# Two score buffers instead of one, and token-sum blocks of x read earlier, in a masked self-attention kernel

## The chip, the cores and the metric

The kernel runs on one core of a Trainium2 chip. A core has five engines that run their own instruction streams and wait for each other by semaphores: PE (matrix products, results only into PSUM), DVE (vector work), ACT (elementwise functions, here above all the exponentials), POOL (here it issues the row gathers and scatters) and SP (here it issues the other transfers). PSUM has eight banks; one bank holds 512 float32 values per partition. Times are device microseconds of one execution; the time of a kernel is the median of its runs.

## The reference

```python
xt = jnp.transpose(x, (0, 2, 1))                    # x: (16, 512, 1024), float32
q = xt @ Wq.T                                       # 512 x 512
qh = q.reshape(B, T, 8, 64).transpose(0, 2, 1, 3)   # 8 heads of 64
scores = scale * jnp.einsum('bhqd,bhkd->bhqk', qh, qh)
logits = (scores * cmask + (1.0 - cmask) * NEG) * rmask
attn = jax.nn.softmax(logits, axis=-1)
ctx = jnp.einsum('bhqk,bhkd->bhqd', attn, qh)
out = ctx.transpose(0, 2, 1, 3).reshape(B, T, D) @ Wo.T
return x + jnp.transpose(out, (0, 2, 1))
```

Queries, keys and values are the same projection. The mask has about half of the 1024 tokens of a batch on. A token that is on attends only to the tokens that are on. A token that is off has logits of zero everywhere, so its row is the plain mean over all tokens of the batch: this is why the kernel needs sums of x over all tokens.

## The kernel before, in words

The kernel sorts the tokens of each batch into slots: the tokens that are on come first, and 512 to 544 slots ("A") are computed. The four blocks of 128 slots are gathered as rows of x (`gather`, an indirect transfer on POOL, tile `xa`), the few slots beyond 512 are the "tail" (tile `xt`). Float32 products are made from float16 halves: each operand is split into a high and a low part, and three products are added.

The 16 batches are worked in a software pipeline, in the loop `for b in range(B + 1)` of `run`. While batch b has its scores and products made, batch b + 1 has its queries made and batch b + 2 is gathered, scaled, split and transposed. Each turn of the loop has eight stages, `st` 0 to 7. A stage is: `scores` of the head pair st // 2 and the half st % 2; then what is listed in `side[st]`; then what is listed in `fill[st]`. PE's order is that of the text, since each product is chained behind the one before (`then`). The other engines' orders come from the framework's scheduler: it goes by the order of the text, but an instruction that is ready while its engine is free can go ahead of earlier ones that aren't. Some work is put into queues with a cost and a due time (`drip`: lines T, D, A, X) and leaves them as the text advances.

`scores` (from L852) makes 12 matmuls for two blocks of 128 keys (k = 0, 1) and two heads (h = 0, 1), three products for each, the six of block 0 first. Each block and head has a PSUM bank of its own, 128 keys x 512 queries. Four exponentials on ACT (L870) follow in the order of the blocks; they write the tiles `p`. All four banks belong to one PSUM tile, `S` (profile name `pss`); the other four banks are the rotating tiles `pm`. The same banks are used by `tail_scores` (the scores of the tail, exponentials on L940), by one transpose in `xt` for the first batch, and by two of the four output products in `last`:

```python
self.S = self.ps_s.tile([P, 4 * 512], F32, tag="s", name="pss")
bank = lambda k, h: self.S[:, (2 * h + k) * 512:(2 * h + k + 1) * 512]
```

`attend(b, p)` multiplies the exponentials of a head pair by the values (tiles `v`); it comes two stages after the pair's first scores. Its last products use `pt` (and `pu` for the wider batches), the tail's exponentials, which go through DRAM (`td`) and come back by SP transfers (L972, L973). The reciprocals of the softmax sums are transposed on PE, copied (`rr`, L1042), written to DRAM (`rd`, L1044) and read back spread over partitions (`rb`, L1053 and L1057); DVE multiplies the result by them in `norm_scale` (L1086).

The values `v` of batch b + 1 come from the query halves `hl` by transposing transfers on SP (L707), two for each head pair; DVE adds the two parts (L719), ACT squares them (L735). The gathered rows are scaled and split into tiles `xs` (two buffers; ACT L626, DVE L627) and transposed by SP into `X` (L628). DVE's `range_now` (L566) reads `X` whole.

The token sums: for batch a = b + 2, x itself lies in DRAM as 512 features x 1024 tokens. `load_all(a, c)` reads the block of 128 features c (512 KB, SP, L541) into a tile `xm`, which has two buffers; `sum_half(a, c)` queues an ACT instruction (L529) that sums each row into a column of `ms2`. When all four are there, `mean_x` (L647, L552, L553) writes the means as one more column of `X`. In batch b the four reads stand in `fill[0]` to `fill[3]` and the four sums in `side[2]` to `side[5]`:

```python
for c in range(DC):
    fill[2 * c // 2].append(L(self.load_all, a, c, None if b else first_top))
    side[c + 2 if b else (2, 2, 3, 4)[c]].append(L(self.sum_half, a, c))
```

Of the kernel before, what the change touches and what calls it, by code (L numbers as in the profile page):

```python
# [10 lines left out]
F32 = mybir.dt.float32  # L11
# [3 lines left out]
AF = mybir.ActivationFunctionType  # L15
# [4 lines left out]
P = 128  # L20
D = 512
T = 1024
H = 8
DK = 64
NP = H // 2
DC = D // P
TB = T // P
SCALE = 0.125
# [23 lines left out]
class Fast:  # L52
# [12 lines left out]
    def __init__(self, ctx, tc, x, x_nat, mask_t, wq_t, wo_t, out):  # L65
        self.tc, self.nc = tc, tc.nc
        self.x, self.x_nat, self.out = x, x_nat, out
        self.B = B = x.shape[0] // T
        self.wide = [512 if b in (0, B - 2, B - 1) else C if b < 5 else 528 for b in range(B)]
        pool = lambda name, bufs, **k: ctx.enter_context(tc.tile_pool(name=name, bufs=bufs, **k))  # L70
        self.const = pool("const", 1)
        self.one = pool("one", 1)
        self.dram = pool("dram", 8, space=bass.MemoryType.DRAM)
        self.ps_s = pool("ps_s", 1, space=PS)
        self.ps_m = pool("ps_m", 4, space=PS)
        self.S = self.ps_s.tile([P, 4 * 512], F32, tag="s", name="pss")
        self.st = {}
        self.last_pe = None
        self.scatters = []
        self.exp, self.pool = [], []  # L80

        self.paced, self.beat = False, None
        self.urgent, self.spare = [], []

        self.lines, self.credit, self.rates = {k: [] for k in RATES}, {k: 0.0 for k in RATES}, dict(RATES)
        self.idle, self.now, self.many, self.pair = 0.0, 0.0, 9, 1
        self.w, self.raw = {}, {}
        self.src = {"q": wq_t, "o": wo_t}
        self.setup(mask_t)
# [503 lines left out]
    def xt(self, b, k):  # L593

        nc, s = self.nc, self.st[b]
        A = s["A"]
        n = P if k < 4 else A - 512
        if k == 0:
            self.need(("r", b - 2))
        if k == 3 and b > 1:  # L600
            self.drip(("x", b), 0.1, lambda: self.mean_x(b), "X", 5.0)
        if n:
            x = s["xa"][k] if k < 4 else s["xt"]
            if b == 0:
                if k == 3:
                    s["cut"] = {}
                    for i, (y, r) in {3: (x, P)}.items():
                        z = s["cut"][i] = self.sb([P, D], F32, "tmp", 2)
                        with self.behind(self.last_xa):
                            nc.scalar.activation(z[:r], y[:r], AF.Copy, scale=self.hit[:r, b, i:i + 1])  # L610
                if k > 2:
                    x = s["cut"][k]
                pt = (self.S[:, :DC * n] if k == 3 else self.pm([P, DC * n])).rearrange("p (c n) -> p c n", c=DC)
                for c in range(DC):
                    self.tr(pt[:, c, :], x[:n, c * P:(c + 1) * P], self.ident[:n, :n])
                self.last_xt = self.pe
                self.xsplit(b, (slice(None), slice(None), slice(k * P, k * P + n)), pt)
            else:
                self.drip(("x", b), 0.9, lambda: self.turn_x(b, k, n, x), "X")
# [232 lines left out]
    def scores(self, b, p, half, between=None):  # L852

        nc, s = self.nc, self.st[b]
        self.sums(b)
        hl = s["hl"][p]
        bank = lambda k, h: self.S[:, (2 * h + k) * 512:(2 * h + k + 1) * 512]
        for k in range(2):
            if between and k:
                between()  # L860
            block = slice((2 * half + k) * P, (2 * half + k + 1) * P)
            for m, (t, u) in enumerate(((0, 0), (0, 1), (1, 0))):
                for h, rows in enumerate((slice(0, DK), slice(DK, P))):
                    self.beat = self.mm(bank(k, h), lhsT=hl[rows, t, block], rhs=hl[rows, u, :512], start=(m == 0), stop=(m == 2)).ins
        self.exp = []
        for k in range(2):
            i = 2 * half + k
            x = self.sb([P, 2, C], F32, "p", PB)
            for h in range(2):
                self.exp = [nc.scalar.activation(x[:, h, :512], bank(k, h), AF.Exp, bias=s["nm"][:, 2 * p + h:2 * p + h + 1], scale=SCALE,  # L870
                                                 accum_out=s["z"][:, 2 * p + h, i:i + 1]).ins]
                s["ps"][p, i, h] = x[:, h]
            if s["nt"]:
                s["blocks"].append((p, i, x))
        self.tail_columns(b)
        self.after(1.7 if b else 4.0)
# [42 lines left out]
    def tail_scores(self, b):  # L919

        nc, s = self.nc, self.st[b]
        A, n = s["A"], s["nt"]
        if not n:
            return
        self.sums(b)
        w = 2 * n
        per = P // w
        for j in range(NP // per):
            o = 1024 * j + 512 - A // 2
            for x, y in self.pieces(o, A):  # L930
                for m, (t, u) in enumerate(((0, 0), (0, 1), (1, 0))):
                    for r in range(per):
                        e = j * per + r
                        self.beat = self.mm(self.S[r * w:(r + 1) * w, o + x:o + y], lhsT=s["tk"][:, e, t, :], rhs=s["hl"][e][:, u, x:y],
                                            start=(m == 0), stop=(m == 2)).ins
        s["tp"] = self.sb([P, 2, C], F32, "p", PB)
        for j in range(NP // per):
            o = 1024 * j + 512 - A // 2
            t = s["tp"][:, j, :A]
            nc.scalar.activation(t, self.S[:, o:o + A], AF.Exp, bias=s["nm"][:, H + j:H + j + 1], scale=SCALE,  # L940
                                 accum_out=s["zt"][:, j:j + 1])
            self.drip(("th", b), 1.0, lambda j=j, t=t: self.tail_halves(b, j, t), "T", 1.0 + 0.9 * j)

# [256 lines left out]
    def last(self, b):  # L1200

        s = self.st[b]
        self.paced = False
        self.attend(b, 3)
        pos = [self.S[:, i * 512:(i + 1) * 512] for i in range(2)] + [self.pm([P, 512]) for _ in range(2)]
        part = lambda i, es: self.product(s["ch"], s["cl"], slice(i * P, (i + 1) * P), pos[i], es)
        part(0, range(3))
        self.recip_last(b, 3)
        part(2, range(3))
        part(1, range(3))  # L1210
        while self.urgent or self.spare:
            self.issue()
        for i in (0, 2, 1):
            self.project(b, i, pos[i], range(3, DC))
        part(3, range(3))
        self.project(b, 3, pos[3], range(3, DC))

    def run(self, flag):
        B = self.B
# [79 lines left out]
        first_top = self.st[0]["top"]  # L1299
# [5 lines left out]
        L = lambda f, *a: lambda: f(*a)  # L1305
        Q = lambda n, e, g: L(self.query, n, e, g)
        for b in range(B + 1):
            o, n, a = b - 1, b + 1, b + 2
# [8 lines left out]
            fill = [[] for _ in range(8)]  # L1317
            side = [[] for _ in range(8)]
# [28 lines left out]
            if n < B:  # L1347
# [40 lines left out]
                if b:  # L1388
                    fill[7] += [L(self.top, n, ALL), L(self.bottom, n, ALL)]
                else:  # L1390
                    fill[7] += [L(self.warm, 40), L(self.top, n, ALL)]
            if a < B:
                self.start(a)
                for c in range(DC):
                    fill[2 * c // 2].append(L(self.load_all, a, c, None if b else first_top))
                    side[c + 2 if b else (2, 2, 3, 4)[c]].append(L(self.sum_half, a, c))
                if not b or any(b == g[0] - 2 for g in groups):
                    fill[0 if b else 1] += [L(self.hot, a)]
                else:
                    side[0] += [L(self.hot, a)]  # L1400
                fill[1 if b else 3] += [L(self.index, a)] + [L(self.gather, a, j) for j in range(5 if self.wide[a] > 512 else 4)]
                for k, st in enumerate((4, 5, 6, 6, 7) if b else (4, 4, 5, 6, 6)):
                    side[st].append(L(self.xt, a, k))
# [43 lines left out]
def general_batch(tc, pools, consts, b, x, mask, out):  # L1447
# [5 lines left out]

    xt = big.tile([P, TB, D], F32, name="g_xt")
    nc.sync.dma_start(out=xt, in_=x[bs].rearrange("o (j p) d -> p (o j) d", p=P))
    cm = big.tile([P, T], F32, name="g_cm")
    nc.scalar.dma_start(out=cm, in_=mask[bs].broadcast_to([P, T]))
# [131 lines left out]
```

## Time and profile before

| | before |
|---|---|
| median of 3 runs | 907.66 us (907.16 to 910.43) |
| profiled execution | 904.99 us |
| its span, first to last instruction | 903.3 us |
| mean granted PE clock | 0.991 |
| PE busy | 867.2 us (96%) |
| DVE busy | 646.9 us (72%) |
| ACT busy | 630.5 us (70%) |
| POOL busy | 295.7 us (33%) |

A row of the wait table reads: engine, tile and line that waited, what ended the wait, total us, times, longest. A row of a window reads: stretch, its length, busy us and number of instructions of PE, PEld (weight loads), DVE, ACT and POOL, granted PE clock, share of the DMA engines, GB/s. A busy PE is one with a matmul in flight; matmuls overlap, so the sum of their durations is more than their busy time. SP has no work of its own: its rows are transfers at the time when they are issued, not when they land.

### The profile page before, as it was taken

To read this page: it belongs to the slowest core of one execution; us is meant where nothing else is said; L and a number is where in the kernel's file an instruction comes from. 1 tells how busy PE (TensorE), PEld (TensorE's weight loads), DVE (VectorE), ACT (ScalarE), POOL (GpSimd) and SP (SyncE) were. 2 spreads that over 40 slices of the span, in tenths; PEclk is the share of its full clock that TensorE was granted. 3 is DMA by queue.
4 is the path that set the end of the run, shared out by engine and by line. 5 is a ranking of instruction groups with operands and counts; after the bars stand their busy time and mean duration, and the time that the engine had idled before them with its cause. 6 is when DMAs were issued, how large, how long until landed. Compare 5 with 4: busy or idle time off the path is not lost.

```text
span 903.3 us, 20115 instructions
## 1 busy us (share of the span) xinstructions
PE 867.2 (96%) x7149; PEld 500.1 (55%) x7149; DVE 646.9 (72%) x2027; ACT 630.5 (70%) x1667; POOL 295.7 (33%) x309
## 2 busy tenths in 40 slices
PE   6788999999999999999999999899999999999896
PEld 5565655556565465655555565464655556464443
DVE  7656877867758677787856888586777877655662
ACT  5868786777767768686866868577676867766640
POOL 3201111222122322243443334242432433345673
PEclk9899999999999999999999999999999999999999
DMA  6957766769769888987979988698996979686652
GB/s 189 251 107 169 160 164 162 167 136 209 178 146 191 196 183 215 201 209 192 228 199 219 198 206 215 152 216 202 200 220 156 220 202 222 166 175 161 204 197 110
DMA packets 193129, 169.24 MB, mean 187 GB/s; under 512 B 145135, under 2 KB 155629, under 8 KB 193021
## 3 DMA queue, kind: packets, MB, share of 16 engines
q1 hardware_dynamic: 171836, 100.20, 52.2%
q0 software_dynamic: 21184, 67.68, 24.8%
q8 instruction: 58, 0.95, 0.5%
q14 instruction: 51, 0.41, 0.2%
HBM read 97.30 MB, written 38.51 MB: 150 GB/s over the span
## 4 chain that ended last, share of the span: by engine, by line
PE 83%; DMA 8%; ACT 4%; DVE 3%; issue 1%; POOL 0%; SPq 0%; POOLq 0%; DVEq 0%; ACTq 0%
PE pm L107 61%; PE pss L107 20%; DMA X<-xs 3%; ACT p L870 2%; PE pm L110 1%; DMA pu<-td 1%; DMA xa<-x_in,idx 1%; DMA pt<-td 1%; DMA rb<-rd 1%; DMA v<-hl 1%; ACT xs L626 0%; POOL xa L492 0%; DVE xa L1178 0%; DVE xs L627 0%; DVE xa L1114 0%
## 5 line engine op out<-in xcount | busy, mean ns | idle before, releaser
L870 ACT ACTIVATE p<-pss,nm 128x512 f32<-128x512 f32 x512 | 346.3, 686 | 149.0 <-PE pss L107 133.5
L107 PE MATMUL pm<-p,v 128*64 128x264 f32 (+2 forms) x2048 | 243.6, 391 | 0.5 <-DVE hl L672 0.4
L107 PE MATMUL pss<-hl 64*128 64x512 f16 x1536 | 193.3, 383 | 10.9 <-ACT p L870 8.4
L107 PEld LDWEIGHTS pm<-p,v 128*64 128x64 f32 x2048 | 141.7, 137 | 95.2 <-issue 16.0
L107 PE MATMUL pm<-X,wqh 128*128 128x264 f16 (+5 forms) x1024 | 177.5, 277 | 2.4 <-DMA X<-xs 2.1
L107 PE MATMUL pm<-X,wql 128*128 128x264 f16 (+5 forms) x512 | 141.6, 276 | 0.0
L492 POOL DMA_INDIRECT xa<-x_in,idx x68 | 71.8, 1055 | 204.0 <-DVE idx L393 70.2
L107 PEld LDWEIGHTS <-hl 64*128 64x128 f16 (+1 forms) x1568 | 69.9, 95 | 100.2 <-issue 36.9
L1191 POOL DMA_INDIRECT y_out<-xa,idx x68 | 70.3, 1034 | 132.6 <-DVE xa L1114 28.3
L107 PEld LDWEIGHTS <-wqh 128*128 128x128 f16 x1024 | 96.7, 98 | 29.8 <-issue 14.9
L870 ACT ACTIVATION_READ_ACCUMULATOR p<-pss,nm 128x1 f32 x512 | 103.9, 203 | 0.0
L1191 POOL DMA_INDIRECT y_out<-xi,idx x56 | 65.4, 1168 | 109.8 <-PE pss L107 30.0
L492 POOL DMA_INDIRECT xi<-x_in,idx x56 | 56.5, 1010 | 114.3 <-PE pss L107 55.4
L107 PE MATMUL pm<-woh,ch 128*128 128x512 f16 x240 | 91.4, 381 | 0.0
L107 PE MATMUL pm<-woh,cl 128*128 128x512 f16 x240 | 91.0, 379 | 0.1
L107 PE MATMUL pm<-wol,ch 128*128 128x512 f16 x240 | 91.0, 379 | 0.0
L672 DVE SCALAR_TENSOR_TENSOR hl<-pm,hl 128x264 f16<-128x264 f32 (+5 forms) x128 | 54.8, 428 | 31.2 <-ACT hl L671 30.8
L107 PEld LDWEIGHTS <-ch 128*128 128x128 f16 x480 | 43.4, 98 | 59.4 <-issue 15.6
L671 ACT ACTIVATE hl<-pm 128x264 f16<-128x264 f32 (+5 forms) x128 | 51.0, 398 | 29.7 <-PE pm L107 29.5
L529 ACT ACTIVATE xm<-xm 128x1024 f32<-128x1024 f32 (+1 forms) x60 | 62.4, 1041 | 2.7 <-DMA xm<-x_nat_in 2.7
L1086 DVE TENSOR_TENSOR c<-c,rb 128x528 f32<-128x528 f32 (+2 forms) x60 | 42.0, 703 | 26.1 <-DMA rb<-rd 24.7
L566 DVE TENSOR_REDUCE top<-X 128x1 f32<-128x529 f16 (+4 forms) x64 | 44.1, 695 | 20.7 <-DMA X<-xs 15.8
(237 smaller groups left out, 1158.6 us busy)
## 6 DMA issues: line engine op xcount, KB each, us to landing
xm<-x_nat_in SPq DMA_DIRECT2D x56, 512.0 KB
rb<-rd SPq DMA_DIRECT2D x28, 512.0 KB
ub<-ud SPq DMA_DIRECT2D x16, 256.0 KB
pt<-td SPq DMA_DIRECT2D x27, 132.0 KB
td<-th SPq DMA_DIRECT2D x9, 264.0 KB
td<-th SPq DMA_DIRECT2D x8, 272.0 KB
pt<-td SPq DMA_DIRECT2D x8, 272.0 KB
xi<-x_nat_in SPq DMA_DIRECT2D x8, 256.0 KB
```

Source lines behind the costliest of these rows:

```text
L107: return self.then(self.nc.tensor.matmul(out, lhsT=lhsT, rhs=rhs, start=start, stop=stop))
L110: return self.then(self.nc.tensor.transpose(out, x, ident))
L492: dma = self.nc.gpsimd.indirect_dma_start(out=tile[:n], out_offset=None, in_=self.x, in_offset=bass.IndirectOffsetOnAxis(ap=idx, axis=0))
L529: self.nc.scalar.activation(s["xm"][k], s["xm"][k], AF.Copy, accum_out=s["ms2"][:, k:k + 1])
L566: self.once(nc.vector.tensor_reduce(s["top4"][:, c:c + 1], self.X[b % 2][:, c, :s["A"] + min(b, 2) % 2 + min(b, 1)], AX.X, ALU.max, apply_ ...
L671: self.last_hl = nc.scalar.activation(hl[:, 0, cols], pq, AF.Copy, scale=1.0 / (SX * SW)).ins
L672: nc.vector.scalar_tensor_tensor(hl[:, 1, cols], pq, 1.0 / (SX * SW), hl[:, 0, cols], ALU.mult, ALU.subtract)
L870: self.exp = [nc.scalar.activation(x[:, h, :512], bank(k, h), AF.Exp, bias=s["nm"][:, 2 * p + h:2 * p + h + 1], scale=SCALE, accum_out=s[" ...
L1086: self.once(nc.vector.tensor_tensor(c[:, :A], c[:, :A], s["rp"][p] if "rp" in s else s["rb"][:, p, :A], ALU.mult), self.beat)
L1191: dma = self.nc.gpsimd.indirect_dma_start(out=self.out, out_offset=bass.IndirectOffsetOnAxis(ap=idx, axis=0), in_=x, in_offset=None)
```

## The change

The one PSUM tile of four banks becomes two tiles of two banks, `S[0]` and `S[1]`, one for each block of 128 keys; within a tile, the bank is that of the head. `tail_scores` uses one of them for each of its runs, and `xt` and `last` use `S[0]`. The number of banks is the same.

For batches from the third on, the reads c = 0 and 1 of batch b + 3 are listed in `fill[6]` and `fill[7]` of turn b, where they stood in `fill[0]` and `fill[1]` of turn b + 1. The reads c = 2 and 3 go from `fill[2]` and `fill[3]` to `fill[1]` and `fill[2]`. The sums go from `side[2]` to `side[5]` to `side[0]`, `side[1]`, `side[3]` and `side[4]`. The first turn keeps its places for batch 2.

```diff
-        self.S = self.ps_s.tile([P, 4 * 512], F32, tag="s", name="pss")
+        self.S = [self.ps_s.tile([P, 2 * 512], F32, tag="s%d" % k, name="pss") for k in range(2)]
...
-                pt = (self.S[:, :DC * n] if k == 3 else self.pm([P, DC * n])).rearrange("p (c n) -> p c n", c=DC)
+                pt = (self.S[0][:, :DC * n] if k == 3 else self.pm([P, DC * n])).rearrange("p (c n) -> p c n", c=DC)
...
-        bank = lambda k, h: self.S[:, (2 * h + k) * 512:(2 * h + k + 1) * 512]
+        bank = lambda k, h: self.S[k][:, h * 512:(h + 1) * 512]
...
-            o = 1024 * j + 512 - A // 2
+            o = 512 - A // 2
...
-                        self.beat = self.mm(self.S[r * w:(r + 1) * w, o + x:o + y], lhsT=s["tk"][:, e, t, :], rhs=s["hl"][e][:, u, x:y],
+                        self.beat = self.mm(self.S[j][r * w:(r + 1) * w, o + x:o + y], lhsT=s["tk"][:, e, t, :], rhs=s["hl"][e][:, u, x:y],
...
-            nc.scalar.activation(t, self.S[:, o:o + A], AF.Exp, bias=s["nm"][:, H + j:H + j + 1], scale=SCALE,
+            nc.scalar.activation(t, self.S[j][:, o:o + A], AF.Exp, bias=s["nm"][:, H + j:H + j + 1], scale=SCALE,
...
-        pos = [self.S[:, i * 512:(i + 1) * 512] for i in range(2)] + [self.pm([P, 512]) for _ in range(2)]
+        pos = [self.S[0][:, i * 512:(i + 1) * 512] for i in range(2)] + [self.pm([P, 512]) for _ in range(2)]
...
+            if a + 1 < B:
+                self.start(a + 1)
+                for c in range(2):
+                    fill[6 + c].append(L(self.load_all, a + 1, c))
             if a < B:
-                self.start(a)
+                if not b:
+                    self.start(a)
                 for c in range(DC):
-                    fill[2 * c // 2].append(L(self.load_all, a, c, None if b else first_top))
-                    side[c + 2 if b else (2, 2, 3, 4)[c]].append(L(self.sum_half, a, c))
+                    if not b or c > 1:
+                        fill[c if not b else c - 1].append(L(self.load_all, a, c, None if b else first_top))
+                    side[(0, 1, 3, 4)[c] if b else (2, 2, 3, 4)[c]].append(L(self.sum_half, a, c))
```

More of the change, by code (lines that the diff above doesn't have):

```diff
@@ L937, in tail_scores @@
         for j in range(NP // per):
-            o = 1024 * j + 512 - A // 2
+            o = 512 - A // 2
             t = s["tp"][:, j, :A]
-            nc.scalar.activation(t, self.S[:, o:o + A], AF.Exp, bias=s["nm"][:, H + j:H + j + 1], scale=SCALE,
+            nc.scalar.activation(t, self.S[j][:, o:o + A], AF.Exp, bias=s["nm"][:, H + j:H + j + 1], scale=SCALE,
                                  accum_out=s["zt"][:, j:j + 1])
```

## The prediction

> **What bounds the kernel.** I read the page's busy line first, then the waits of the matrix engine (PE), then single stretches of the timeline. The timeline's columns are start, duration, engine, line, operation, tiles, form, count, and in brackets the idle time before it with what ended it.
>
> ```profile
> PE 867.2 (96%) x7149; PEld 500.1 (55%) x7149; DVE 646.9 (72%) x2027; ACT 630.5 (70%) x1667; POOL 295.7 (33%) x309
> PE pss L107 <- ACT p L870: 8.4, 5, 3.1
> 33.50:89.00 55.50, 44.84 (x397) 28.10 (x397) 34.75 (x114) 44.00 (x115) 4.65 (x5) 0.91 0.73 159
> 260.00:580.00 320.00, 313.55 (x2588) 178.02 (x2586) 238.28 (x761) 232.29 (x610) 108.58 (x107) 1.00 0.86 202
> 580.00:835.80 255.80, 255.80 (x2062) 145.41 (x2058) 182.54 (x558) 182.82 (x490) 97.34 (x92) 0.99 0.80 192
> ```
>
> PE is busy 867.2 of 903.3 us and its matmuls stay as they are, so nearly all that can be won are its 36.1 us of idle time. The three windows show where that lies: 10.7 us in the first batch, 6.5 us between 260 and 580, nothing from there to 835.8; the rest is the start before the first scores and the last batch with the end. PE's waits for the exponentials (8.4 us in five) are the largest entry; the single waits follow.
>
> **Part 1, the two score buffers.** First what one tile of four banks does now, in the last batch:
>
> ```profile
> 850.78 1.47 PE L107 MATMUL pss<-hl 64*128 64x512 f16 x12
> 852.17 1.09 PE L107 MATMUL pm<-ident,rcol 128*64 128x128 f32 x16
> 855.18 1.47 PE L107 MATMUL pss<-hl 64*128 64x512 f16 x12 [1.92 <-ACT p L870]
> 845.77 1.47 PE L107 MATMUL pss<-hl 64*128 64x512 f16 x12 [0.24 <-ACT p L870]
> 850.89 0.37 ACT L988 COPY c<-pm 128x256 f32<-128x256 f32 x1 [0.50 <-PE pm L107]
> 852.35 0.69 ACT L870 ACTIVATE p<-pss,nm 128x512 f32<-128x512 f32 x1 [1.09 <-PE pss L107]
> 853.03 0.68 ACT L870 ACTIVATE p<-pss,nm 128x512 f32<-128x512 f32 x1
> 854.35 0.69 ACT L870 ACTIVATE p<-pss,nm 128x512 f32<-128x512 f32 x1
> 89.03 0.82 PE L107 MATMUL pss<-hl 64*128 64x512 f16 x6 [0.42 <-ACT p L870]
> ```
>
> The exponentials begin at 852.35, after all twelve matmuls (850.78 + 1.47 = 852.25), and the next scores begin 0.14 us after the fourth exponential (854.35 + 0.69 = 855.04). So the whole tile is handed over at once, both ways. With a tile for each block, the first pair of exponentials waits for six matmuls (0.82 us with the drain, so 0.65 us sooner), and the first six matmuls of the next stage wait for two exponentials. Here: ACT is free at 851.26, so the exponentials start 0.65 sooner; the second ends at 853.06, the fourth at 854.39. PE is free at 853.26, starts there, does six, waits from 853.91 to 854.39 + 0.14 = 854.53, and ends at 855.35 where it now ends at 856.65: 1.30 us won. The 0.24 before 845.77 goes as well. Together 1.5 us.
>
> In the first batch the same happens:
>
> ```profile
> 42.14 2.75 PE L107 MATMUL pss<-hl 64*128 64x512 f16 x12 [3.08 <-ACT p L870]
> 51.20 0.39 PE L107 MATMUL pm<-X,wqh 128*128 128x274 f16 x2 [2.10 <-DMA X<-xs]
> 75.29 0.67 ACT L870 ACTIVATE p<-pss,nm 128x512 f32<-128x512 f32 x1
> 76.89 0.70 ACT L870 ACTIVATE p<-pss,nm 128x512 f32<-128x512 f32 x1
> 77.73 2.75 PE L107 MATMUL pss<-hl 64*128 64x512 f16 x12 [2.73 <-ACT p L870]
> 79.55 0.72 ACT L626 ACTIVATE xs<-xa,hs 128x512 f16<-128x512 f32 x1 [1.07 <-DMA X<-xs]
> ```
>
> The 3.08 before 42.14 brings nothing: whatever PE wins there it loses at 51.20, where it waits for a transfer that does not depend on these scores. The 2.73 before 77.73 splits. Six matmuls can follow the second exponential (75.29 + 0.67 = 75.96, plus 0.14), the other six still start at 77.73; the end comes at 78.55 and not at 80.48. These twelve took 2.75 us where the others take 1.47, at half rate, and two short stalls with work between may leave the rate whole. But the next exponentials stand behind the split of x at 79.55, which waits for a transfer, so of the 1.9 us some 1.5 remain when the first batch ends. Bounds: 0, if that transfer sets everything, and 4.8 (2.73 + 0.42 + 1.28 + the slow start behind it). I take 1.5, nearest to the worked rows. Part 1 is 3.0 us.
>
> The Trainium skill, page "TensorE: Matmul & The Clock Gate", section "What's actually happening", says that the half rate comes after about one idle window of 3.4 us. The trace differs: half rate after 3.08 and 2.73 us, none after 2.10. By the page's figure the 1.28 us at 77.73 would have another cause and could stay.
>
> The price of part 1 is a wait in the middle of each stage's scores, on ACT. Two starts of six take 2 x 0.82 against 1.47, so 0.17 x 128 = 22 us is the upper end, if the pipeline drains at each; the lower end is 0, if a wait that is already met costs nothing. I take 0, since in most stages the old exponentials are over long before. Behind that wait stands all of PE's queue. On ACT, the first exponentials move forward by 0.65 us in all 128 stages; between 260 and 835 that is cover without value, as PE is full.
>
> **Part 2, the reads of x.** Two of four 512 KB reads per batch move from stages 0 and 1 to stages 6 and 7 of the batch before in the text, the other two one stage forward; the sums move with them. What the SP queue does today is not the text's order:
>
> ```profile
> 524.50 0.39 PE L107 MATMUL pss<-hl 64*128 64x512 f16 x2
> 530.07 1.26 SPq L1053 DMA_DIRECT2D rb<-rd  x2
> 532.75 1.01 SPq L972 DMA_DIRECT2D pt<-td  x2
> 559.84 0.36 SPq L541 DMA_DIRECT2D xm<-x_nat_in  x1
> 560.30 1.23 SPq L707 DMA_TRANSPOSE v<-hl  x1
> 570.93 9.26 SPq L628 DMA_TRANSPOSE X<-xs  x3
> 567.27 0.69 DVE L719 TENSOR_TENSOR v<-v 128x512 f32<-128x512 f16 x1 [3.44 <-DMA v<-hl]
> 577.54 0.72 ACT L626 ACTIVATE xs<-xt,hs 16x512 f16<-16x512 f32 x1 [4.01 <-DMA X<-xs]
> 578.16 0.68 ACT L940 ACTIVATE p<-pss,nm 128x528 f32<-128x528 f32 x1
> 578.98 2.29 PE L107 MATMUL pss<-hl 64*128 64x512 f16 x12 [2.43 <-ACT p L940]
> 581.61 4.40 PE L107 MATMUL pm<-p,v 128*64 128x264 f32 x32
> 498.79 3.78 PE L107 MATMUL pm<-p,v 128*64 128x264 f32 x32
> DVE v L719 <- DMA v<-hl: 21.0, 10, 3.5
> ```
>
> The read of the next batch already goes out at 559.84, five stages early, as soon as a buffer is free: just ahead of the last transpose of v (560.30). DVE then stands 3.44 us for that v, the split of x behind it is late, so is the transpose at 570.93, ACT stands 4.01 us for it, and PE 2.43 us. The restart costs 2.29 - 1.47 = 0.82 in the scores and 4.40 - 3.78 = 0.62 in the products behind: 3.9 us in all. DVE waits like this in ten batches (21.0 us), and one batch earlier the late transpose came out another way:
>
> ```profile
> 476.23 0.70 DVE L566 TENSOR_REDUCE top<-X 128x1 f32<-128x529 f16 x1 [3.75 <-DMA X<-xs]
> 470.68 0.39 PE L107 MATMUL pss<-hl 64*128 64x512 f16 x2
> 481.45 1.13 SPq L972 DMA_DIRECT2D pt<-td  x2
> 477.18 0.39 PE L107 MATMUL pm<-X,wqh 128*128 128x264 f16 x2 [0.29 <-DVE rr L1042]
> 491.50 0.39 PE L107 MATMUL pm<-pt,vt 96*128 96x264 f16 x2 [1.94 <-DMA pt<-td]
> ```
>
> There DVE waited for X, the row of reciprocals and pt went out late, and PE lost 0.29 + 1.94 = 2.2 us. With the sums in stages 0, 1, 3 and 4, the buffers come free one to two stages sooner, the two early reads go out before the last v, and both stalls go: 3.9 + 2.2 = 6.1 us. Bounds: 0 if a read still stands before v, 6.1 if none does; I take the upper end, as DVE's 3.44 us is about one 512 KB read (2.6 us at the 202 GB/s of the window). What is late next at 578.98 is not seen up to 835.
>
> What it costs: the other two reads now come in stages 1 and 2, where the reciprocals (rb), pt and the first v transposes run. On SP they may pass those transposes, whose sums on DVE come some stages later; POOL's queue is not passed, but its gathers share the DMA engines, and those are at 0.86 of their time in the window 260 to 580 above:
>
> ```profile
> 278.59 0.27 PE L107 MATMUL pm<-pu,vt 64*128 64x272 f16 x1 [1.19 <-DMA pu<-td]
> L529 ACT ACTIVATE xm<-xm 128x1024 f32<-128x1024 f32 x56 | 59.9, 1070 | 0.6 <-DMA xm<-x_nat_in 0.6
> ```
>
> If the read goes ahead of pt, PE waits. From 470.68 to pt's issue at 481.45 are 10.8 us, and PE waited 1.94; from 524.50 to 532.75 are 8.3, and it did not. So 2.5 us later costs up to 1.9, and the upper end is 12 batches x 2.0 = 24 us; the lower is 0, if pt goes first, as it does in the text. I take 2.6 us, one read's time, once, in the batch that has no slack (278.59, where PE already waits 1.19). The sums add 2 x 1.07 us to ACT in stages 0 and 1, with its 70% no bound there.
>
> **Sum.** The profiled execution took 904.99 us (span 903.3). 904.99 - 3.0 - 6.1 + 2.6 = 898.5. The median before, 907.66, is 2.67 above that execution, so I predict 901.2.
>
> **Rivals.**
> - Only part 1 shows. The reads go out when buffers are free and not where the text has them, so one may still stand ahead of the last v: 907.66 - 3.0 = 904.7, within 0.5%. For it: the read at 559.84, five stages ahead of its text. Against: the sums, which free the buffers, do move.
> - Slower: the read of stage 1 goes out ahead of rb and pt. SP stands idle before rb at 530.07, which invites it. Then 12 x 2.0 replaces the 2.6: 922.6; in half of the batches it gives 910.6. It decides from 0.8 us a batch on (9.1 / 12). Against: the sum that frees the buffer comes after the exponentials of stage 0, at about the time of rb. The Trainium skill, page "DMA: Bandwidth & Descriptors", section "Queues, rings and completion order", says that each DMA engine takes a ring's descriptors in order; this rival is that rule at work, and 560.30 behind 559.84 agrees with it.
> - The wait inside the scores drains PE: +22 us, 923. Against: only that the old exponentials are mostly over by then; no row shows a met wait inside a run of scores.
>
> **How the numbers follow.** The forecast, both parts at work, has 0.50, with a range of its own of 897 to 903. Only part 1: 0.25. The reads ahead of pt: 0.20, of which 0.13 in so many batches that it is slower by over 0.5%. The drained scores: 0.05. The low end is all gains at their bounds, 907.66 - 4.8 - 1.5 - 6.1, about 895; the high end, 911, takes in pt late in half of the batches. A change under 0.5%, or 4.5 us, is about what can't be told from none. Faster: 0.50; within: 0.25 + 0.07 = 0.32; slower: 0.13 + 0.05 = 0.18.
>
> **What the new profile would show.** Part 1: exponentials starting 0.65 us before the twelve matmuls end, no wait near 855 over 0.7 us. Part 2: DVE's total wait for v well under 21.0, no wait of PE for L940. Wrong: more waits of PE for pt or pu, longer waits of DVE for rb, or pairs of six matmuls taking 1.64.

## The result and the profile after

The changed kernel takes 917.77 us (median; 910.6 to 926.14) against 906.35 us for the kernel before on the same chip: 1.0115 times the time, with a 95% interval of 1.008 to 1.015. The forecast was 901.2 us and faster; it is slower by some 10 us (0.0115 of 906.35), beyond the upper end of the range, 911. The kernel was run again with the experiments: 916.2 against 903.66 us, 1.0127 (1.0092 to 1.0162). One of the first six executions, the profiled one of 926.14 us, was disturbed, so the ratio leaves it out and the rows of the changed kernel below are those of the second run, whose span is 915.3 us against 903.3 before.

The busy line of the page, and the largest waits of PE:

```profile
PE 873.8 (95%) x7149; PEld 498.4 (54%) x7149; DVE 645.5 (71%) x2027; ACT 628.8 (69%) x1667; POOL 305.5 (33%) x309
```

```profile
PE pm L107 <- DMA pt<-td: 5.0, 3, 2.5
PE pss L107 <- ACT p L870: 4.2, 5, 1.8
PE pm L110 <- DVE smcol L793: 4.0, 1, 4.0
...
PE pm L110 <- DVE p L890: 2.8, 3, 1.6
```

PE's wait for the exponentials went from 8.4 to 4.2 us, as part 1 said. New are a wait of 4.0 us for `smcol` (the largest of a head's sums of squares) and waits for `p` at L890; `pt` went from 1.9 to 5.0 us. PE is also 6.6 us longer busy (873.8 against 867.2) with the same 7149 matmuls. Windows by stretch of work, the kernel before first, show where the time went; the borders are the starts of batches 0, 1, 2, 8, 10 and 15:

```profile
33.50:89.00 55.50, 44.84 (x397) 28.10 (x397) 34.75 (x114) 44.00 (x115) 4.65 (x5) 0.91 0.73 159
89.00:144.50 55.50, 55.47 (x455) 32.42 (x454) 43.72 (x128) 43.59 (x113) 8.40 (x8) 1.00 0.65 151
144.50:470.70 326.20, 324.30 (x2635) 183.84 (x2636) 243.51 (x776) 236.79 (x621) 93.30 (x92) 1.00 0.81 189
470.70:579.00 108.30, 103.63 (x867) 59.03 (x867) 80.82 (x263) 77.55 (x204) 38.88 (x38) 1.00 0.90 205
579.00:835.80 256.80, 256.80 (x2068) 145.92 (x2067) 183.54 (x562) 182.82 (x490) 97.34 (x92) 0.99 0.80 192
835.80:903.30 67.50, 58.16 (x431) 29.16 (x430) 36.12 (x89) 25.81 (x75) 40.28 (x37) 0.98 0.52 170
```

```profile
33.60:89.10 55.50, 43.45 (x399) 26.93 (x400) 34.75 (x113) 43.50 (x114) 6.16 (x5) 0.96 0.70 159
89.10:151.90 62.80, 60.29 (x458) 33.76 (x459) 43.83 (x129) 44.28 (x115) 8.08 (x8) 0.92 0.61 138
151.90:478.00 326.10, 325.10 (x2633) 183.10 (x2632) 245.00 (x776) 235.91 (x621) 97.80 (x92) 1.00 0.82 188
478.00:589.10 111.10, 105.91 (x867) 59.37 (x868) 80.63 (x265) 77.40 (x204) 39.32 (x37) 0.98 0.88 200
589.10:848.80 259.70, 256.60 (x2069) 144.66 (x2068) 181.86 (x561) 182.09 (x490) 98.67 (x93) 1.00 0.82 190
848.80:915.30 66.50, 58.33 (x431) 28.73 (x431) 35.19 (x87) 25.66 (x75) 42.52 (x37) 0.97 0.52 173
```

Batch 1 is 7.3 us longer, the two batches where the forecast saw gains 2.8 longer instead of shorter, the full stretch 2.9 longer; the last batch is 1.0 shorter. Batch 1 is the plainest case. The matmuls around its start, and two windows behind it:

```profile
74.48 0.82 PE L107 MATMUL pss<-hl 64*128 64x512 f16 x6 [1.23 <-ACT p L870]
75.81 0.82 PE L107 MATMUL pss<-hl 64*128 64x512 f16 x6 [0.51 <-ACT p L870]
...
88.68 0.45 PE L110 MATMUL pm<-ident,smcol 128*128 128x128 f32 x1 [4.00 <-DVE smcol L793]
```

```profile
88.70:92.70 4.00, 3.88 (x16) 1.34 (x16) 2.09 (x13) 1.85 (x5) 0.00 (x0) 0.50 0.02 4
92.70:96.70 4.00, 4.00 (x25) 2.34 (x27) 2.67 (x5) 3.14 (x11) 0.00 (x0) 0.66 0.11 26
```

Where 2.73 us stood before the scores at 77.73, there are now 1.23 and 0.51, and the scores run at full rate (0.82 us for six). But the gain does not reach the next batch: PE comes sooner to a product for which DVE is not ready, stands 4.00 us in one piece (still inside the first batch's window, whose length stays 55.5 us), and then has a clock of 0.50 for 4 us and of 0.66 for 4 more, which is worth 4.0 x 0.50 + 4.0 x 0.34 = 3.4 us in batch 1. The Trainium skill, page "TensorE: Matmul & The Clock Gate", section "What's actually happening", says half rate after an idle window of about 3.4 us; this wait agrees with it, shorter ones shown below do not.

The rest of batch 1's 7.3 us is a second stall, for the tail's exponentials:

```profile
114.74 0.41 PE L107 MATMUL pm<-pt,vt 128*128 128x272 f16 x2 [2.04 <-DMA pt<-td]
...
115.72 2.57 PE L107 MATMUL pss<-hl 64*128 64x512 f16 x11
```

```profile
113.00:121.00 8.00, 5.92 (x37) 3.32 (x38) 3.64 (x12) 4.37 (x12) 2.05 (x2) 0.79 1.06 148
```

PE waits 2.04 us for `pt` and 0.34 for `pu`, and the clock of 0.79 takes another 8.0 x 0.21 = 1.7 us: 3.4 + 2.4 + 1.7 = 7.5, about what the window shows.

The last batch did what was forecast: its wait of 1.92 us is 0.51.

```profile
866.96 0.82 PE L107 MATMUL pss<-hl 64*128 64x512 f16 x6 [0.51 <-ACT p L870]
```

On DVE two waits have grown, before and after:

```profile
DVE rcol L1021 <- ACT p L870: 13.7, 14, 1.0
DVE sd L738 <- ACT tmp L735: 11.3, 12, 3.6
```

```profile
DVE rcol L1021 <- ACT p L870: 43.3, 17, 4.8
DVE sd L738 <- ACT tmp L735: 33.6, 31, 2.7
```

`rcol` at L1021 is the first step of the softmax sums and needs the last exponential of a batch; `sd` at L738 is the sum of ACT's squares over a head's 64 values (the expectations below call it a maximum). DVE waits 30 and 22 us longer at these two. At `rcol` most of that is an old wait in a new place: DVE's wait at the maximum `m` (L802) for PE falls from 22.4 to 0.9 us, since DVE now stands at the sums first. Nothing in the text of the change concerns these instructions. The order in which DVE's instructions stand has changed: with the two buffers alone, 365 of 2027 instructions of DVE, 74 of 1065 of ACT and 18 of 455 of SP have to be moved to get from one order to the other (the fewest that do it).

### The profile page after: what moved, and what is told of

It reads as the page before. It is cut to its first block, busy times and chain, and to the rows that moved or that the text cites. A ratio compares the mean times of both kernels' runs of the same rounds, so it can differ in the third digit from the quotient of the medians.

```text
span 924.4 us, 20160 instructions
## 1 busy us (share of the span) xinstructions
PE 877.8 (95%) x7149; PEld 501.0 (54%) x7149; DVE 646.3 (70%) x2027; ACT 628.5 (68%) x1667; POOL 301.9 (33%) x309
## 4 chain that ended last, share of the span: by engine, by line
PE 67%; DMA 13%; DVE 8%; ACT 6%; issue 3%; POOL 1%; SPq 1%; POOLq 0%; DVEq 0%; ACTq 0%
PE pm L107 50%; PE pss L107 16%; ACT p L870 3%; DMA X<-xs 3%; DMA rb<-rd 3%; DMA v<-hl 3%; PE pm L110 1%; DMA xa<-x_in,idx 1%; DMA pt<-td 1%; ACT xm L529 1%; ACT xs L626 1%; DMA pu<-td 1%; DVE xs L627 1%; DVE v L719 1%; DVE top L566 1%
## 5 line engine op out<-in xcount | busy, mean ns | idle before, releaser
L870 ACT ACTIVATE p<-pss,nm 128x512 f32<-128x512 f32 x512 | 344.8, 687 | 83.3 <-PE pss L107 54.1
L107 PE MATMUL pm<-p,v 128*64 128x264 f32 (+2 forms) x2048 | 247.8, 396 | 3.6 <-DVE hl L672 3.6
L492 POOL DMA_INDIRECT xa<-x_in,idx x68 | 77.1, 1134 | 210.7 <-DVE idx L393 66.7
L870 ACT ACTIVATION_READ_ACCUMULATOR p<-pss,nm 128x1 f32 x512 | 105.0, 205 | 0.0
L1191 POOL DMA_INDIRECT y_out<-xi,idx x56 | 61.5, 1099 | 121.5 <-PE pm L107 49.9
L492 POOL DMA_INDIRECT xi<-x_in,idx x56 | 60.9, 1088 | 107.6 <-PE pss L107 47.0
L988 ACT COPY c<-pm 128x264 f32<-128x264 f32 (+2 forms) x128 | 43.2, 383 | 54.2 <-PE pm L107 54.0
L738 DVE TENSOR_REDUCE sd<-tmp 128x8 f32<-128x512 f32 x64 | 43.7, 683 | 32.6 <-ACT tmp L735 32.1
L671 ACT ACTIVATE hl<-pm 128x264 f16<-128x264 f32 (+5 forms) x128 | 47.4, 396 | 28.1 <-PE pm L107 28.0
```

Of the source, the lines that this page charges most:

```text
L107: return self.then(self.nc.tensor.matmul(out, lhsT=lhsT, rhs=rhs, start=start, stop=stop))
L492: dma = self.nc.gpsimd.indirect_dma_start(out=tile[:n], out_offset=None, in_=self.x, in_offset=bass.IndirectOffsetOnAxis(ap=idx, axis=0))
L671: self.last_hl = nc.scalar.activation(hl[:, 0, cols], pq, AF.Copy, scale=1.0 / (SX * SW)).ins
L738: nc.vector.tensor_reduce(s["sd"][:, e, :], sq.rearrange("p (k d) -> p k d", d=DK), AX.X, ALU.add)
L988: nc.scalar.copy(c[:, g * CH:(g + 1) * CH], po[g])
L1191: dma = self.nc.gpsimd.indirect_dma_start(out=self.out, out_offset=bass.IndirectOffsetOnAxis(ap=idx, axis=0), in_=x, in_offset=None)
```

## The experiments

All are ratios to the kernel before on the same chip, with 95% intervals. Lines of code that were added shift the line numbers by up to 29 in some profiles (L870 is L899 there).

| | ratio | interval |
|---|---|---|
| whole change, again | 1.0127 | 1.0092 to 1.0162 |
| two buffers only | 1.0091 | 1.0059 to 1.0123 |
| reads only | 1.0001 | 0.9969 to 1.0033 |
| two buffers, orders of ACT, DVE and SP kept | 0.9958 | 0.9934 to 0.9982 |
| one tile, new orders | 1.0161 | 1.0126 to 1.0195 |
| whole change, orders of reads only | 0.9978 | 0.9952 to 1.0004 |
| two buffers, ACT's order kept | 1.0068 | 1.0044 to 1.0092 |
| before, one swap on DVE | 1.0068 | 1.0043 to 1.0092 |
| two buffers, maximum first | 1.0043 | 1.0018 to 1.0069 |
| two buffers, DVE's order kept | 1.0009 | 0.9983 to 1.0036 |
| two buffers, SP's order kept | 1.0133 | 1.0100 to 1.0167 |
| whole change, maximum first | 1.0100 | 1.0064 to 1.0137 |
| two buffers, orders kept but the swap | 0.9958 | 0.9936 to 0.9981 |
| two buffers, ACT and DVE kept, SP new | 0.9999 | 0.9970 to 1.0028 |
| two buffers, ACT and SP kept, DVE new | 1.0128 | 1.0089 to 1.0168 |
| two buffers, orders kept but 48 sums of squares early | 0.9993 | 0.9961 to 1.0026 |
| two buffers, DVE new but these sums late | 1.0085 | 1.0056 to 1.0114 |

### The two parts apart

Three kernels: the change again; the buffers only, with the reads and sums of the kernel before; the reads only, with its one tile. In terms of the diff above:

```diff
 # buffers only: the hunks of the score tiles, and the last hunk as before
...
-                for c in range(2):
-                    fill[6 + c].append(L(self.load_all, a + 1, c))
...
 # reads only: the last hunk, and one score tile as before
-        self.S = [self.ps_s.tile([P, 2 * 512], F32, tag="s%d" % k, name="pss") for k in range(2)]
+        self.S = self.ps_s.tile([P, 4 * 512], F32, tag="s", name="pss")
```

The theories at the start: A, the buffers change the order of the other engines and that order costs; B, the reads cost.

> The changed kernel once more, for a profile beside the parts. Its ratio to the kernel before was 1.0115 (1.008 to 1.015): if that holds on this chip too, 1.008 to 1.015 again, some 10 us. If the loss was that of one chip, 0.995 to 1.005.

> Part 1 alone: two score buffers, the reads and sums of x as before. The prediction's term: 3.0 us faster (ratio 0.997). Theory A (the buffers change the order of ACT's and DVE's instructions, and that order makes the new waits): slower, 1.005 to 1.012, with ACT waiting for products at L988 in more than 40 us in all, against 19.5 before. Theory B (the loss is from the reads): 0.994 to 1.000, L988 near 20 us.

> Part 2 alone: reads and sums of x early, one score tile. The prediction's term: 3.5 us faster (6.1 won, 2.6 lost; ratio 0.996). Theory A: 0.995 to 1.002. Theory B: 1.006 to 1.015, with new waits of PE for pt or for work behind the sums on ACT.

The loss comes with the buffers, 1.0091. The reads alone are 1.0001, no change. Of B nothing is left. A's sign at L988 is there (41.4 us with the buffers alone), but a wait of ACT for products need not cost anything, so A had to be tested on the order itself. (It is 41.4 us in the kernel of the next section too, which is faster: it was no sign of the loss.)

The reads' own rows are worth a look, since they show the forecast of part 2 come true and be paid for in part. In this profile (span 900.8, so 2.5 us shorter than the one before, where the medians don't differ):

```profile
492.12 0.39 PE L107 MATMUL pm<-pt,vt 96*128 96x264 f16 x2 [0.48 <-DMA pt<-td]
577.43 1.47 PE L107 MATMUL pss<-hl 64*128 64x512 f16 x12
277.67 1.14 PE L107 MATMUL pm<-p,v 128*64 128x272 f32 x8 [1.07 <-DVE hl L672]
```

The stall of 1.94 us for `pt` is 0.48, and the one of 2.43 us for L940 is gone. In their place PE waits 1.07 and 0.82 us in two earlier batches for DVE's second half of a query, which stands on DVE behind a wait for `rb` (26.6 us in all, 24.7 before). The wait of 1.19 us for `pu` at 278.59 is gone.

### The order kept, and the order alone

The framework orders each engine's instructions by its own model of time. To separate that order from the buffers, the order of one kernel was written down and forced on the other by edges that are meant to set order and add no wait. The text of both is the same instruction for instruction, so the lists fit; POOL's order is left to the framework. What the edges alone cost or win (the kernel before with its own lists) was not run.

```diff
+    def keep(self):
...
+        for e, shift in order.items():
+            mine = [i for i in block if i.engine == of[e] and "Boundary" not in type(i).__name__]
...
+            row = [mine[k + d] for k, d in enumerate(shift)]
+            for x, y in zip(row, row[1:]):
+                self.tc.add_manual_dep(y, x.name, mybir.DependencyInfo(mybir.DependencyClass.NoSync, mybir.DependencyReason.DATA),
...
```

(`shift` is the other kernel's order, as offsets from the order of the text.)

Four kernels: two buffers with the lists of the kernel before; the kernel before with the lists of the two buffers; the whole change with the lists of the reads-only kernel; two buffers with ACT's list of the kernel before alone, where the framework orders DVE and SP anew.

> Two score buffers, reads as before, and every instruction of ACT, DVE and SP in the order of the kernel before (edges that set order and no wait). Theory A, the order of those engines costs the time: 0.995 to 1.001, near the predicted 3.0 us won, no wait of PE of 4 us for smcol at the end of the first batch. Theory C, the buffers themselves cost it (a wait in the middle of the scores, exponentials that start sooner): 1.006 to 1.012, as with the buffers alone.

> The reverse: one score tile of four banks, and ACT, DVE and SP in the order that the kernel with two buffers has. Theory A: 1.006 to 1.013, with DVE's wait of ACT's squares (L738) near 30 us and the wait for smcol at the end of the first batch. Theory C: 0.997 to 1.003.

> The whole change, and ACT, DVE and SP in the order that the reads-only kernel has. Theory A: both terms of the prediction show, 0.992 to 0.999 (6.5 us won by the terms: 0.993). Theory C: 1.006 to 1.013, as the whole change.

> Two score buffers, reads as before, and ACT alone in the order of the kernel before; DVE and SP are ordered anew behind that. If ACT's order (74 of 1065 instructions moved) is what costs: 0.995 to 1.002. If DVE's own order is (365 of 2027 moved, 326 still so here): 1.005 to 1.012.

Theory A holds on both sides. Two buffers with the old orders are faster, 0.9958: 3.8 us (1.6 to 6.0), where the forecast had 3.0 for part 1. The new orders with the old tile are slower, 1.0161, above the 1.013 that theory A allowed (interval from 1.0126). So the buffers as such are a gain, and the orders that come with them cost 0.9958 to 1.0091, some 12 us. In the kernel with the old orders the wait at the end of the first batch is 1.36 us, batch 1 has its full clock, and DVE's two waits are down to 7.7 and 5.2 us:

```profile
87.51 0.30 PE L139 MATMUL pm<-ident,smcol 128*128 128x128 f32 x1 [1.36 <-DVE smcol L822]
```

```profile
87.70:143.20 55.50, 55.50 (x458) 32.40 (x457) 44.11 (x129) 44.84 (x115) 8.67 (x8) 1.00 0.66 153
```

```profile
DVE sd L767 <- ACT tmp L764: 7.7, 7, 3.5
...
DVE rcol L1050 <- ACT p L899: 5.2, 14, 0.4
```

The whole change with the orders of the reads-only kernel is 0.9978, 2.0 us won (-0.4 to 4.3) where both terms would give 6.5; part 2 adds nothing to part 1 here either. ACT's order kept alone leaves 1.0068: most of the loss is not in ACT's order.

### One swap

The most regular difference on DVE: in the kernel before, the maximum `m` (L802), for which PE's next small product waits, stands one place ahead of the sums `rcol` (L1021). With the buffers the sums stand first. Theory D takes this as the cause, theory E says that many moves share it. One run puts the swap alone into the kernel before; another takes it out of the kernel with two buffers, by an edge (`self.maxima` holds the instruction of L802; the `m` of these lines is a view of `rcol`):

```diff
-            nc.vector.tensor_tensor(m, s["z"][:, lo:hi, :], more, ALU.subtract)
+            with self.behind(*self.maxima):
+                nc.vector.tensor_tensor(m, s["z"][:, lo:hi, :], more, ALU.subtract)
```

In the first, DVE's list differs in 15 places like this one:

```diff
-  p L890, m L802, rcol L1021, xa L1114
+  p L890, rcol L1021, m L802, xa L1114
```

Two more keep, on two buffers, the order of DVE alone or of SP alone by its list. The last puts the edge into the whole change.

> The kernel before, all orders as they are, but in 15 batches two neighbours on DVE change places: the first step of the softmax sums (rcol, L1021) stands ahead of the maximum m (L802) and no longer behind it. Theory D (this one swap carries the loss): the sums wait for the last exponential, m stands behind it and PE behind m, some 0.6 us in each of 13 batches as with the one tile in the new order, so 1.006 to 1.011. Theory E (the loss is spread over many moves): 1.000 to 1.004.

> Two score buffers, reads as before, and one edge in each batch that keeps the sums (L1021) behind the maximum (L802); 28 instructions of DVE move by it, ACT and SP stay as with the buffers alone. Theory D: 0.995 to 1.002. Theory E: 1.004 to 1.010.

> Two score buffers, and DVE alone in the order of the kernel before; ACT (62 moved) and SP (22 moved, the reads of x ahead of the transposes of v in 13 batches) are ordered anew. If DVE's order is what costs: 0.995 to 1.001. If SP's or ACT's is: 1.004 to 1.010.

> Two score buffers, and SP alone in the order of the kernel before, so that the reads of x go behind the transposes of v where they did; DVE and ACT as with the buffers alone. If the reads ahead of v cost it: 0.996 to 1.002. If not: 1.006 to 1.012, as with the buffers alone.

> The whole change, and the one edge in each batch that keeps the sums (L1021) behind the maximum (L802); 28 instructions of DVE move by it, nothing else. With the buffers alone the edge gave back 0.0048 of the ratio (1.0091 to 1.0043). If it does the same here: 1.0127 - 0.0048 = 1.008, between 1.005 and 1.011. If the early reads make another wait carry the loss: 1.010 to 1.016. If the swap is all of it: 0.995 to 1.003.

The swap alone costs the kernel before 0.0068, 6.1 us, in 15 batches. Its profile shows how, on DVE and then on PE:

```profile
738.23 0.19 DVE L1050 TENSOR_TENSOR rcol<-z,zc 128x32 f32<-128x32 f32 x1 [1.32 <-ACT p L899]
738.34 0.28 DVE L831 TENSOR_REDUCE m<-pm 128x1 f32<-128x128 f32 x1
```

```profile
738.77 0.36 PE L136 MATMUL pm<-ident,m 128*128 128x8 f32 x2 [0.59 <-DVE m L831]
```

```profile
PE pm L136 <- DVE m L831: 8.7, 15, 0.6
```

The sums wait 1.32 us for the last exponential, the maximum stands ready behind them, PE stands 0.59 us for the maximum, and this comes back in 15 batches. The Trainium skill, page "PSUM — Partial Sum Buffer", section "Engine vs sequencer instructions", says that VectorE's queue is strictly first in, first out; these rows agree. Taking the swap out of the kernel with two buffers brings 1.0091 to 1.0043, about half of the way to no loss, with intervals that just overlap; in the whole change 1.0127 to 1.0100, less than the intervals can tell apart. DVE's whole order kept gives 1.0009, SP's order kept gains nothing (1.0133). These two also show that PE's wait for `smcol`, the plainest one above, does not carry most of the loss: with DVE's order kept it is 3.9 us, with SP's kept, where the loss is whole, 1.4. First the one, then the other:

```profile
PE pm L136 <- DVE smcol L819: 3.9, 1, 3.9
```

```profile
PE pm L121 <- DVE smcol L804: 1.4, 1, 1.4
```

### Where the rest of the order's cost lies

Again lists, on two buffers: the old ones with only the swap on DVE; the old ones for ACT and DVE, SP ordered anew; the old ones for ACT and SP, for DVE the one that it has with the buffers alone.

> Two score buffers, all orders of the kernel before, and only the one swap on DVE in 15 batches (sums ahead of the maximum). The swap cost 0.0068 with one tile; with two the last exponential is over 0.65 us sooner, so the sums may have nothing to wait for behind which PE stands. If the swap costs with two buffers what the edge gave back (0.0048): 0.9958 + 0.0048 = 1.0006, between 0.998 and 1.004. If the sooner exponentials cover it: 0.994 to 0.998.

> Two score buffers, ACT and DVE in the order of the kernel before, SP ordered anew (21 moved, the reads of x among them). Against 0.9958 with all three kept: if SP's order carries the rest of the loss, 1.000 to 1.006; if not, 0.994 to 0.999.

> Two score buffers, ACT and SP in the order of the kernel before, DVE in the order that it has with the buffers alone (365 moved). If DVE's order carries nearly all of the loss: 1.006 to 1.013. If ACT's and SP's do: 0.996 to 1.003.

The swap, on two buffers with everything else in the old order, costs nothing: 0.9958, as without it. In the batch shown above the sums now wait 0.66 us, and PE's product follows with no wait:

```profile
726.57 0.19 DVE L1050 TENSOR_TENSOR rcol<-z,zc 128x32 f32<-128x32 f32 x1 [0.66 <-ACT p L899]
726.68 0.28 DVE L831 TENSOR_REDUCE m<-pm 128x1 f32<-128x128 f32 x1
```

```profile
727.11 0.36 PE L136 MATMUL pm<-ident,m 128*128 128x8 f32 x2
```

Where the maximum stands first, the sums' wait shows how much later the last exponential comes. In the same batch it is 1.02 us in the kernel before, and 0.37 with two buffers and the orders kept:

```profile
734.39 0.19 DVE L1021 TENSOR_TENSOR rcol<-z,zc 128x32 f32<-128x32 f32 x1 [1.02 <-ACT p L870]
```

```profile
732.79 0.19 DVE L1050 TENSOR_TENSOR rcol<-z,zc 128x32 f32<-128x32 f32 x1 [0.37 <-ACT p L899]
```

So theory D falls as the whole explanation: the exponentials that end 0.65 us sooner pay for this swap, whose wait of PE was 0.59. What the edge gave back with the buffers alone (0.0048) is then not this swap's own price: it hangs on other moves, or is partly noise. The totals of DVE's waits mislead here: at the sums DVE waits 36.0 us in this kernel, which loses nothing, and 40.4 in the one with one tile, which loses 0.0068.

DVE's new order with the others kept is 1.0128, all of the loss, and SP's alone 0.9999, which is 0.004 over 0.9958, with intervals that overlap. The next suspect was DVE's other long wait: 48 of the 64 sums of squares (L738) stand one to five places earlier in the new order. Theory F takes them as the carriers, theory G sees many moves together. One run moves them in the old list, one moves them back in the new one; a place of the first:

```diff
-  c L1086, c L1087, hl L672, cth L1098, v L719, ctl L1099, sd L738
+  c L1086, sd L738, c L1087, hl L672, cth L1098, v L719, ctl L1099
```

> Two score buffers, all orders of the kernel before, and on DVE only the 48 maxima of squares (L738) that the new order has earlier go ahead of the same neighbours (hl L672, c L1087, v L719, xa L1114 and others). Theory F (these carry DVE's loss: each waits for ACT's square with the neighbours behind it): 1.004 to 1.013, DVE's wait for squares near 30 us. Theory G (many moves together): 0.995 to 1.001.

> The reverse: two score buffers, ACT and SP in the order of the kernel before, DVE in its new order (1.0128), but the 48 maxima of squares (L738) go back behind the neighbours. Theory F: 0.996 to 1.003, DVE's wait for squares near 8 us. Theory G: 1.005 to 1.013.

Put into the old order, the early sums of squares bring DVE's wait for ACT's squares from 7.7 to 37.5 us and the ratio from 0.9958 to 0.9993. Taken out of the new order, they bring it from 1.0128 to 1.0085, and another instruction takes the wait over (37.1 us, from 7.6):

```profile
DVE sd L767 <- ACT tmp L764: 37.5, 38, 3.5
```

```profile
DVE xs L656 <- ACT xs L655: 37.1, 23, 2.9
```

About 0.004 either way (the intervals overlap, but both runs go the same way), a quarter of what DVE's order costs (1.0128 less 0.9958). Theory F's full price does not hold; G is nearer. Which of the other moves carry the rest was not tried one by one and stays open.

## Why the prediction was wrong

**What bounds the kernel** stands: PE is the bound, and its idle time is where time was won and lost.

**Part 1, the stalls.** Right in kind, and near in sum partly by luck. With the orders kept the whole measured 3.8 us (1.6 to 6.0) against the term of 3.0; by places, in its profile, batch 1 starts 1.3 us sooner (87.74 against 89.03; forecast 1.5) and the last batch is 1.7 us shorter (forecast 1.5). The last batch's wait was worked out as 0.62 us (853.91 to 854.53) and is 0.51 in the changed kernel. The stall at 77.73 split into two, as said. But the 1.3 us at the end of the first batch are made of two errors that nearly cancel. The 3.08 us before 42.14 were to bring nothing, as PE would wait at 51.20 for a transfer that does not depend on these scores; with the orders kept PE is past that wait at 50.48, and it comes to the scores of 84.69 2.4 us sooner. Then a wait that was not foreseen, 1.36 us for `smcol`, takes about half of that back. What the clock rule of the Trainium skill (page "TensorE: Matmul & The Clock Gate", section "What's actually happening") left open, whether the slow scores at 77.73 had another cause, the rows settle: at 74.48 and 75.81 they take 0.82 us for six, full rate, once the waits ahead of them are short.

**Part 1, the price.** The wait in the middle of the scores, taken as 0, is 0: the 1536 score matmuls have a mean of 382 ns with two buffers and the orders kept, and 383 before, and the idle time of PE before all of them is 8.5 us, against 10.9.

```profile
L136 PE MATMUL pss<-hl 64*128 64x512 f16 x1536 | 193.7, 382 | 8.5 <-ACT p L899 5.4 <-ACT p L969 3.1
```

**The step that failed** is the last sentence of that part: "On ACT, the first exponentials move forward by 0.65 us in all 128 stages; between 260 and 835 that is cover without value, as PE is full." On the chip it is so: with the orders kept, the stretch from batch 2 to the start of the last batch takes 691.7 us, and 691.3 before. But the orders of ACT, DVE and SP are made before the run, and with the two buffers 365 instructions of DVE stand elsewhere. That the framework's model saw the same 0.65 us and moved them for it is our reading; the model's times were not read. The account of the kernel said that an instruction that is ready can go ahead of earlier ones that are not; the working priced the old order with new times. The term that is missing is the new order, +0.0133 of the ratio or about 12 us (1.0091 less 0.9958). Of the 17 us between the 6.5 won by forecast and the 10.4 lost, these are 12, and the net of part 2, below, is 3.5.

**The first batch.** The 1.5 us were bounded by "the split of x at 79.55, which waits for a transfer". In the changed kernel another thing was late next, `smcol`, and it cost more than it took back: the clock was down for 8 us behind its 4.0 us. As shown, this wait does not carry most of the loss.

**Part 2.** In the reads alone the two stalls went as worked out (0.48 us left of 1.94, none of 2.43), and DVE's wait for v fell to 16.6 us from 21.0, less than "well under". In the whole change the first stall is back, 2.48 us for `pt` at 500.22, behind a wait of 1.10 us for the reciprocals `rr`. The net of -3.5 us was not there: 1.0001, or -2.8 to +3.0 us. Two reasons show, though no run separates them. New waits came in the batches before (1.07 and 0.82 us). And the 6.1 us were read off one execution, as if its stalls were the kernel's. That they may not be is suggested by two other kernels, both with two buffers, the old orders and the reads where they were: the profile of the first has both stalls, and the profile of the second, which differs by the 15 swaps, has neither there and one of the second kind elsewhere. They are two programs, so this is a hint and no proof. First the one, then the other:

```profile
488.64 0.39 PE L136 MATMUL pm<-pt,vt 96*128 96x264 f16 x2 [2.60 <-DMA pt<-td]
578.32 0.61 PE L136 MATMUL pss<-hl 64*128 64x512 f16 x2 [3.07 <-ACT p L969]
```

```profile
624.29 0.39 PE L136 MATMUL pss<-hl 64*128 64x512 f16 x2 [1.90 <-ACT p L969]
```

**The rivals.** Reads ahead of `pt` stood in the sum once (2.6 us), and in the rival in every batch (922.6 us). A read goes out ahead of `pt` in one batch only, batch 1, both in the reads alone and in the whole change (the first two rows, then the other two):

```profile
101.92 0.34 SPq L541 DMA_DIRECT2D xm<-x_nat_in  x1
...
104.07 1.24 SPq L972 DMA_DIRECT2D pt<-td  x2
```

```profile
106.30 0.34 SPq L541 DMA_DIRECT2D xm<-x_nat_in  x1
107.57 1.25 SPq L972 DMA_DIRECT2D pt<-td  x2
```

In the reads alone PE does not wait for it there, so the term was 0 and not 2.6. In the whole change it is the batch where PE stands 2.04 us for `pt`; whether the read or the late batch around it did that stays open. The drained scores are excluded by the 382 ns and the 8.5 us. That only part 1 would show was right of the reads and missed the order. None named the order of the other engines: the chance of 0.18 for slower hung on drained scores, which did not come, and on reads ahead of `pt`, which came once.

## What to carry to other kernels

Where a framework orders the engines by a model, a change that makes one instruction ready sooner is a change of every order behind it: compare the orders before pricing the change. Keep the old order by edges if the comparison shows moves; here that turns a loss of 0.9% into a gain of 0.4% with the same two buffers. Don't look for the costly moves by the total waits of an engine that is not the bound: the same wait of some 36 to 40 us of DVE stood in a kernel that lost nothing and in one that lost 0.7%. And look for a stall in a second execution before counting it as the kernel's.

## What the runs showed of the hardware

A wait of 4.00 us of PE is followed by a clock of 0.50 for 4 us and 0.66 for the next 4, so it costs nearly twice its length (4.0 + 3.4); a wait of 1.36 us at the same place costs itself alone. How long a wait may be is not one number: in the changed kernel twelve score matmuls take 2.80 us, half rate, behind a wait of only 1.75 us that follows one of 1.58 us and one of 0.23, and eleven take 2.57 us behind the waits of 2.04 and 0.34 shown above. But six take 0.82 us, full rate, behind waits of 1.23 and 0.51 there, and behind 1.82 and 0.80 with the orders kept.

```profile
38.31 0.23 PE L107 MATMUL pm<-id,hl 128*128 128x128 f16 x1 [1.58 <-ACT hl L671]
...
40.86 2.80 PE L107 MATMUL pss<-hl 64*128 64x512 f16 x12 [1.75 <-ACT p L870]
```

The other surprise is how much 15 exchanges of two neighbours can do: with one tile, two instructions of 0.2 and 0.3 us in the other order cost 0.7% of the kernel.
